# The last 512 tokens of a four-layer sequence model as two chunks of 256, with the later layers as one stream beside the later attention

## The chip, the cores and the metric

The kernel runs on one core of a Trainium2 chip. The metric is the device time of one execution in microseconds (us); three runs were timed, and the median is quoted. Beside these there is one profiled execution, whose trace gives start, duration and cause of waiting of every instruction. The engines are called as the profile calls them: PE (TensorE matmul) and PEld (its weight loads), DVE (VectorE), ACT (ScalarE), POOL (GpSimd) and SP (SyncE, which here only issues DMAs).

## The reference

The input `x` has 2 sequences of 1024 tokens with 256 features, all in f32. Four layers follow one another, each adding to `x`; the kernel normalizes the tokens (layer norm) ahead of each.

```
attention   16 heads of 128; softmax(min/max-clipped q.k/sqrt(128) + causal mask + slope_h * key) v, then Wo
ternary FFN weights rounded to -1/0/1 times a scale per group of 64; silu(g) * u, rms norm, projection 1024 -> 256
state space in-projection 256 -> 2 x 512, causal convolution over 4 tokens, silu; delta = softplus(...);
            for 512 channels x 16 states:  h[t] = exp(delta[t] a) h[t-1] + delta[t] B[t] x[t];  y[t] = sum_n C[t] h[t]
            y gated by silu(z), out-projection
2:4 FFN     silu(g) * u with 1024 hidden units; of every four the two of largest magnitude are kept; projection
```

Attention needs all earlier tokens of its sequence (keys and values), the state space needs the state and three convolution inputs of the token before. The other layers work on each token by itself.

## The kernel before

**Chunks.** The 2048 tokens are cut into four chunks of 512, `CH = [(0,0),(0,1),(1,0),(1,1)]` (sequence, half). `x[k]` stays in SBUF. A chunk's attention must be finished for all 16 heads before its other three layers, `rest(k)`, can begin.

**Attention** (`attention`, L382) is a generator that goes through the heads of all chunks in order and yields after each tile of 128 queries. For one tile, `scores` (L355) multiplies q with all keys so far (`s`, L362), clips and masks on DVE (`ss`, L366), adds the slope and finds the extreme (`nm`, L372, DVE, reads `ss` and `alibi` from SBUF), and exponentiates on ACT (L377). Two tiles later `turn` (L293) transposes the tile on PE, and a copy on ACT or DVE (`pT`, L296) brings it back; when a head's four tiles are turned, `values` (L304) and one tile later `project` (L318, L324 on DVE) follow. `qkv` (L335, L342) makes the next head's q, k, v during the second tile. Keys and values of a sequence's first half are written to DRAM (`kd`, `vd`) and loaded again for each head of the second half (L282, L283). A head's four weights, its slope row, and the old keys and values are loaded by SP (L267 to L283), each as soon as a buffer is free.

**The other layers** are generators too. `ternary_ffn` (L451), `state_space` (L517) and `kept_two_ffn` (L885) yield numbers that stand for cost. The state space has 64 products per chunk, one for each of 4 channel groups and 16 states, each on tiles of 128 channels x 512 tokens: SP loads rows of B and C from DRAM to all partitions (`bs`, `cs`, L691), POOL makes `db` = du * bs (L736), ACT makes `da` = exp (L750) into PSUM, DVE scans (`hs`, L757) and keeps the last column as `carry` (L766), POOL weighs `hc` = hs * cs (L771), and PE adds `hc` into `y` by transposing matmuls (L701). For the last chunk (`tail_end`) `db` is made by PE instead, with diagonal matrices (L730) or scaled copies (L724), so that POOL has only `hc`.

**Order.** The first attention chunk runs beside the quantizing of the ternary weights. Then, for k = 1, 2, 3, the tiles of attention k are dealt out against `rest(k-1)` in proportion to the yielded costs, a product counting 2.2, and what is left of `rest(k-1)` is emptied before the next chunk:

```
for k in range(1, len(CH)):
    r, done = rest(k - 1), 0.0
    for i in range(H * UT):
        next(heads)
        whole = cost(k - 1)
        while done < whole * (i + 1) / (H * UT):
            done += next(r, whole)
    for _ in r:
        pass
```

`rest(3)` runs alone at the end. To fill its gaps, the four last projections of `rest(2)` are held back (`held`, `fill_in`) and handed out there. A scheduler turns this order of emission into one order per engine, and allocates buffers from pools with a fixed number of each tag; each engine then works strictly in its order.

Of the kernel before, what the change touches and what calls it, by code (L numbers as in the profile page):

```python
# [17 lines left out]
P = 128  # L18
# [11 lines left out]
U = 512  # L30
UT = U // P
NU = S // U
# [9 lines left out]
def kernel(  # L42
# [28 lines left out]
    def bank(tag, bufs):  # L71
        return lambda name, dt=F32: ps.tile([P, 512], dt, tag=tag, name=name, bufs=bufs)
# [6 lines left out]
    CH = [(b, u) for b in range(B) for u in range(NU)]  # L79
    x = []  # L80
    for k in range(len(CH)):
        x.append(const.tile([P, UT, D], F32, name=f"x{k}"))

    def load_x(k):
        b, u = CH[k]
        src = x_in[b, u * U : (u + 1) * U, :].rearrange("(t p) d -> p t d", p=P)
        if k:
            nc.sync.dma_start(out=x[k], in_=src)
        else:

            for t in range(0, UT, 2):
                (nc.scalar if t else nc.sync).dma_start(out=x[k][:, t : t + 2, :], in_=src[:, t : t + 2, :])
# [19 lines left out]
    def layernorm_T(k, key, put, bank):  # L112
# [4 lines left out]
        step = 2 if k == len(CH) - 1 and key[0] != "a" else UT  # L117

        def turn_two(i):
            if i and step == 2:  # L120
                fill_in()
            tp = bank(f"lnp_{key}_{i}").rearrange("p (c t) -> p c t", c=KC)
            for j in range(2):
# [9 lines left out]
            put(slice(i * P, (i + 2) * P), tp)  # L133

        for i in range(UT):
# [3 lines left out]
            if (i + 1) % step == 0:  # L139
# [3 lines left out]
                for j in range(done.start, done.stop, 2):  # L143
                    turn_two(j)

    def plain(pool, key):
        xT = pool.tile([P, KC, U], F32, tag="xT", name=f"xT_{key}")
        return xT, lambda t, p: nc.any.tensor_copy(xT[:, :, t], p)  # L148
# [78 lines left out]
    def normed(k):  # L227
        xns[k], put = plain(a2, f"a{k}")
        layernorm_T(k, f"a{k}", put, ps_mm)
# [32 lines left out]
    def load_head(k, h):  # L262
        b, u = CH[k]
# [8 lines left out]
        n = (u + 1) * U  # L272
# [7 lines left out]
        if u:  # L280
            kd, vd = kept.pop((b, h))
            nc.sync.dma_start(out=w["kT"][:, :U], in_=kd)  # L282
            nc.sync.dma_start(out=w["v_all"][:, :UT, :], in_=vd)  # L283
        return w

    def turn(k, h, j, s, st):

        qi = CH[k][1] * UT + j
# [9 lines left out]
    def values(k, h, st):  # L298
        u = CH[k][1]
        zp = ps_z(f"z_{k}_{h}")  # L300
        last = (u + 1) * UT - 1
        for kb in range(last + 1):
            q0 = max(0, kb - u * UT) * P
# [4 lines left out]
        st["z"] = a2.tile([P, U], F32, tag="z", name=f"zs_{k}_{h}")  # L308
        nc.any.tensor_copy(st["z"], zp)  # L309

    def project(k, h, st):

        rr = a3.tile([P, UT], F32, tag="rr", name=f"rr_{k}_{h}")
        nc.vector.reciprocal(rr, st["rs"])
        for t in range(0, UT, 2):
# [12 lines left out]
    def qkv(k, h, st, xT):  # L328
        u = CH[k][1]
        st["qT"] = a2.tile([P, U], F32, tag="qT", name=f"qT_{k}_{h}")  # L330
        kT = st["kT"][:, u * U : (u + 1) * U]
        for n, dst, scale in (("q", st["qT"], -1.0 / math.sqrt(DH)), ("k", kT, 1.0)):
            pp = ps_mm(f"p{n}_{k}_{h}")
# [5 lines left out]
        vp = ps_mm(f"pv_{k}_{h}").rearrange("p (t m) -> p t m", t=UT)  # L339
        for t in range(UT):  # L340
# [5 lines left out]
        v = st["v_all"][:, u * UT : (u + 1) * UT, :]  # L346
        nc.any.tensor_copy(v, vp)
        if u < NU - 1:
            kd = dr.tile([P, U], F32, tag="kd", name=f"kd_{k}_{h}", bufs=H)
            nc.sync.dma_start(out=kd, in_=kT)  # L350
            vd = dr.tile([P, UT, DH], F32, tag="vd", name=f"vd_{k}_{h}", bufs=H)
            nc.sync.dma_start(out=vd, in_=v)
            kept[CH[k][0], h] = kd, vd

    def scores(k, h, j, st):  # L355

        W = (CH[k][1] * UT + j + 1) * P
# [24 lines left out]
    def attention():  # L382
# [7 lines left out]
        for i, (k, h) in enumerate(heads):  # L390
            st = live.pop(0)
            if i + 1 < len(heads):
                live.append(load_head(*heads[i + 1]))
            u = CH[k][1]
            st["pts"] = [
                a3.tile([P, 4, U], F32, tag="pT", name=f"pT_{k}_{h}_{i}") for i in range(u + 1)
            ]
            st["rs"] = a3.tile([P, UT], F32, tag="rs", name=f"rs_{k}_{h}")
            for j in range(UT):
                s = scores(k, h, j, st)  # L400
                later.append((LAG, lambda a=(k, h, j, s, st): turn(*a)))
                if j == UT - 1:
                    later.append((LAG, lambda a=(k, h, st): values(*a)))
                    later.append((LAG + 1, lambda a=(k, h, st): project(*a)))
                if j == UT - 1 and h == H - 1:
# [8 lines left out]
                if j == 1 and i + 1 < len(heads):  # L414
                    qkv(*heads[i + 1], live[0], xns[heads[i + 1][0]])
                if j == 0 and h == H - 1 and k + 1 < len(CH):

                    with tc.issue_after(tiles[-UT].ins) if k == 0 else nullcontext():
                        normed(k + 1)
                yield k  # L420
# [14 lines left out]
    def glu(pool, key, xTs, g_of, u_of, ic, h, bank=ps_r):  # L435

        g_ps, u_ps = bank(f"g_{key}_{ic}"), ps_r(f"u_{key}_{ic}")
# [7 lines left out]
        sg = pool.tile([P, U], F32, tag="sg", name=f"sg_{key}_{ic}", bufs=2)  # L445
# [5 lines left out]
    def ternary_ffn(k):  # L451
        with ExitStack() as fctx:
# [8 lines left out]
            x2 = [fc.tile([P, KC, U], F32R, name=f"x{i}_{k}") for i in "hl"]  # L461
# [7 lines left out]
            h2 = [fc.tile([P, NFC, U], F32R, name=f"h{i}_{k}") for i in "hl"]  # L469
            ss = fc.tile([P, U], F32, name=f"ss_{k}")  # L470
            for ic in range(NFC):
                h = f2.tile([P, U], F32, tag="h", name=f"h_{k}_{ic}")
# [7 lines left out]
                lower = nc.vector if k == len(CH) - 1 else nc.gpsimd  # L480
# [3 lines left out]
                else:  # L484
                    sq = f2.tile([P, U], F32, tag="sq", name=f"sq_{k}_{ic}")
# [4 lines left out]
            for t in range(UT):  # L490
# [4 lines left out]
            inv = f2.tile([P, UT], F32, tag="inv", name=f"inv_{k}")  # L495
            nc.vector.tensor_scalar(inv, sp[:, :UT], 1.0 / FF, RMS_EPS, ALU.mult, ALU.add)
            nc.gpsimd.tensor_tensor(inv, inv, minus_half[:, :UT], ALU.pow)
            for t in range(UT):
# [18 lines left out]
    def state_space(k):  # L517
        b, u = CH[k]
        first, last, tail_end = u == 0, u == NU - 1, k == len(CH) - 1
# [3 lines left out]
        with ExitStack() as mctx:  # L523
# [3 lines left out]
            xs = mc.tile([P, NDC, U], F32, name=f"xs_{k}")  # L527
            sz = mc.tile([P, NDC, U], F32, name=f"sz_{k}")
            dtl = mc.tile([P, U], F32, name=f"dtls_{k}")
            work = lambda name: mc.tile([P, U], F32, tag="cv", name=name, bufs=2)  # L530
            diag = mc.tile([P, DN, UT, P], F32, name=f"diag_{k}") if tail_end else None
# [6 lines left out]
            bcd = dr.tile([2, DN, U], F32, tag="bcd", name=f"bcd_{k}", bufs=2)  # L538

            row_of = lambda tag, name, bufs: mc.tile([P, U], F32, tag=tag, name=name, bufs=bufs)  # L540
# [3 lines left out]
            def steps(c):  # L544

                vp = ps_r(f"dt_{k}_{c}")
# [30 lines left out]
            def turned(c, du):  # L577

                tp = ps_r(f"dup_{k}_{c}")
                for t in range(UT):  # L580
# [8 lines left out]
            with ExitStack() as ictx:  # L589
# [11 lines left out]
                xT, put = plain(mi, f"m{k}")  # L601
# [3 lines left out]
                def in_proj(e):  # L605
                    pp = (spare(k) if e % 2 else ps_r)(f"in_{k}_{e}")
# [7 lines left out]
                for e in range(NDC):  # L614
                    xp = mi.tile([P, DC - 1 + U], F32, tag="xp", name=f"xp_{k}_{e}", bufs=2)
# [5 lines left out]
                    if not last:  # L621
                        nc.gpsimd.tensor_copy(tail[:, e, :], xp[:, U:])
                    acc = work(f"cv_{k}_{e}")
                    nc.vector.tensor_scalar(acc, xp[:, 0:U], cw(e, 0), None, ALU.mult)
                    for i in range(1, DC):
                        nc.vector.scalar_tensor_tensor(
                            acc, xp[:, i : i + U], cw(e, i), acc, op0=ALU.mult, op1=ALU.add
# [9 lines left out]
                dl_ps = ps_r(f"dtl_{k}")  # L637
# [8 lines left out]
                bc_ps = ps_da(f"bcp_{k}")  # L646
# [8 lines left out]
                bc = mi.tile([2 * DN, U], F32, name=f"bc_{k}", padded_shape=[P, U])  # L655
# [3 lines left out]
                if tail_end:  # L659
                    turns[0] = turned(0, parts[0][1])  # L660

                    bT_ps = ps_da(f"bT_{k}")[:, : UT * 2 * DN].rearrange("p (t n) -> p t n", t=UT)
# [385 lines left out]
```

## Time and profile before

| | |
|---|---|
| timed runs | 1835.65 us median (1833.6, 1835.65, 1840.51) |
| profiled execution, first to last instruction (span) | 1836.9 us, inside the range of the timed runs |
| instructions | 24217 |
| busy: PE / DVE / ACT / POOL | 94% / 66% / 52% / 45% of the span |
| mean granted clock of PE | 0.989 of full |
| DMA | 255.99 MB, 139 GB/s on average |

From the start times of the instructions, the span falls into these stages. Attention 0 ends at about 236 us, attention 1 at 733, attention 2 at 1121, attention 3 at 1606. The scans (L757) of the four chunks run from 345 to 564, from 823 to 997, from 1234 to 1452, and, in the last stage without attention, from 1672 to 1776. Busy time of PE is an average that hides these stages: a matmul's end is modelled, and a run of matmuls counts as busy from the first to the last.

### The profile page before, as it was taken

What the parts mean: (1) busy time and instruction counts of PE and PEld (TensorE: products, weight loads), DVE (VectorE), ACT (ScalarE), POOL (GpSimd) and SP (SyncE); (2) the same over time, 40 slices, a digit from 0 to 9 for tenths busy, and PEclk for the clock granted to TensorE, in tenths of its full rate; (3) what the DMA queues carried; (4) which work ended last, traced back from release to release, by engine and by line L of the source; (5) the groups of instructions that cost most, each with busy time, mean ns of one, the idle gap of its engine ahead of it and who ended that gap; (6) DMA issues with size and microseconds to landing.
All of it is one profiled execution on the core that took longest, in us unless ns stands there. A gap on an engine that the chain in (4) does not pass through costs nothing. (4 is left out here: it accounts for less than half of the span.)

```text
span 1836.9 us, 24217 instructions
## 1 busy us (share of the span) xinstructions
PE 1718.3 (94%) x7956; PEld 1144.2 (62%) x7956; DVE 1218.3 (66%) x2349; ACT 963.7 (52%) x1789; POOL 832.2 (45%) x674
## 2 busy tenths in 40 slices
PE   7999999998999999998888999999999999998899
PEld 4666666555656557755555667756656565566895
DVE  5666555777785473458886565557788655667975
ACT  3444474656563553555554545566555446446742
POOL 3324032588892000419998000418898500035870
PEclk9999999999999999999999999999999999999999
DMA  6443512466662311337787324227665430212541
GB/s 201 128 142 128 193 46 88 149 203 204 216 202 91 103 52 48 125 109 232 245 247 224 116 71 141 82 67 228 226 214 184 142 115 26 75 53 86 178 136 57
DMA packets 178301, 255.99 MB, mean 139 GB/s; under 512 B 16240, under 2 KB 90992, under 8 KB 177152
## 3 DMA queue, kind: packets, MB, share of 16 engines
q1 hardware_dynamic: 176752, 241.61, 41.4%
q0 software_dynamic: 1152, 12.58, 1.9%
q8 instruction: 63, 1.03, 0.2%
q14 instruction: 62, 0.51, 0.1%
q10 hardware_dynamic: 272, 0.26, 0.0%
HBM read 232.04 MB, written 22.35 MB: 138 GB/s over the span
## 5 line engine op out<-in xcount | busy, mean ns | idle before, releaser
L771 POOL TENSOR_TENSOR hc<-hs,cs 128x512 f32<-128x512 f32 x256 | 362.1, 1428 | 10.8 <-DVE ss L366 3.1
L362 PE MATMUL s<-kT,qT 128*128 128x512 f32 (+3 forms) x768 | 302.7, 495 | 19.9 <-DVE ss L366 18.0
L377 ACT ACTIVATE ss<-ss,nm 128x128 f32<-128x128 f32 (+7 forms) x256 | 198.8, 776 | 183.5 <-DVE nm L372 174.1
L366 DVE SCALAR_TENSOR_TENSOR ss<-s,lower 128x512 f32<-128x512 f32 (+3 forms) x384 | 204.6, 549 | 121.0 <-PE s L362 119.4
L736 POOL TENSOR_TENSOR db<-du,bs 128x512 f32<-128x512 f32 x192 | 259.2, 1356 | 44.4 <-DVE hs L757 30.6
L304 PE MATMUL z<-pT,v 128*128 128x512 f32 (+3 forms) x768 | 264.5, 492 | 10.9 <-ACT pT L296 10.2
L372 DVE CUSTOM_DVE_ANT_0 ss<-ss,alibi 128x128 f32<-128x128 f32 (+7 forms) x256 | 241.3, 945 | 3.5
L750 ACT ACTIVATE da<-dl,a_neg 128x512 f32<-128x512 f32 x256 | 177.9, 698 | 115.6 <-DVE hs L757 90.6
L304 PEld LDWEIGHTS z<-pT,v 128*128 128x128 f32 x768 | 142.8, 190 | 145.1 <-issue 92.7
L296 ACT COPY pT<-pt 128x512 f32<-128x512 f32 (+3 forms) x321 | 145.4, 474 | 162.0 <-PE pt L293 160.4
L293 PE MATMUL pt<-ident,ss 128*128 128x128 f32 x1152 | 180.3, 279 | 32.1 <-DVE x L324 18.5
L293 PEld LDWEIGHTS pt<-ident,ss 128*128 128x128 f32 x1152 | 140.0, 142 | 94.7 <-DVE x L324 33.0
L362 PEld LDWEIGHTS s<-kT,qT 128*128 128x128 f32 x768 | 127.9, 193 | 84.1 <-issue 43.4
L757 DVE TENSOR_TENSOR_SCAN hs<-da,db 128x512 f32<-128x512 f32 x128 | 153.8, 1210 | 38.6 <-ACT da L750 20.8
L757 DVE TENSOR_TENSOR_SCAN hs<-da,carry,db 128x512 f32<-128x512 f32 x128 | 159.1, 1269 | 24.4 <-POOL hc L771 14.7
L324 DVE SCALAR_TENSOR_TENSOR x<-o,rr,x 128x256 f32<-128x256 f32 x256 | 108.9, 476 | 76.7 <-PE o L318 76.5
L701 PE MATMUL y<-ident,hc 128*128 128x128 f32 x1024 | 144.8, 279 | 8.4 <-POOL hc L771 8.4
L342 PEld LDWEIGHTS pv<-wv,xT_a 128*128 128x128 f32 x1024 | 124.4, 192 | 37.1 <-issue 25.3
L342 PE MATMUL pv<-wv,xT_a 128*128 128x128 f32 x1024 | 125.8, 275 | 5.5 <-ACT zs L309 3.4
L701 PEld LDWEIGHTS y<-ident,hc 128*128 128x128 f32 x1024 | 121.0, 145 | 14.3 <-POOL hc L771 11.9
L318 PE MATMUL o<-wo,zs 128*128 128x256 f32 x512 | 125.4, 386 | 4.1 <-ACT kT L338 3.0
L335 PE MATMUL pq<-xT_a,wq 128*128 128x512 f32 x256 | 122.7, 601 | 0.7 <-ACT xT_a L148 0.7
(204 smaller groups left out, 2468.7 us busy)
## 6 DMA issues: line engine op xcount, KB each, us to landing
cs<-bcd SPq DMA_DIRECT2D x256, 256.0 KB, 3.8
bs<-bcd SPq DMA_DIRECT2D x192, 256.0 KB, 4.3
alibi<-alibi_d SPq DMA_DIRECT2D x32, 512.0 KB, 4.2
wq<-in_wqT_dram SPq DMA_DIRECT2D x64, 128.0 KB, 3.5
wk<-in_wkT_dram SPq DMA_DIRECT2D x64, 128.0 KB, 3.1
wv<-in_wvT_dram SPq DMA_DIRECT2D x64, 128.0 KB, 2.8
wo<-in_woT_dram SPq DMA_DIRECT2D x64, 128.0 KB, 2.8
alibi<-alibi_d SPq DMA_DIRECT2D x32, 256.0 KB, 3.6
```

Source lines behind the costliest of these rows:

```text
L293: nc.tensor.transpose(tp[:, i, :], s[:, (kb0 + i) * P : (kb0 + i + 1) * P], ident)
L304: nc.tensor.matmul(zp[:, q0:], lhsT=st["v_all"][:, kb, :], rhs=st["pts"][kb // 4][:, kb % 4, q0:], start=(kb == 0), stop=(kb == last),)
L342: nc.tensor.matmul(vp[:, t, :], lhsT=xT[:, c, t * P : (t + 1) * P], rhs=st["v"][:, c, :], start=(c == 0), stop=(c == KC - 1),)
L362: nc.tensor.matmul(sp[:, :n], lhsT=st["qT"][:, j * P : (j + 1) * P], rhs=st["kT"][:, k0 : k0 + n], start=True, stop=True,)
L366: nc.vector.scalar_tensor_tensor(s[:, k0 : k0 + n], sp[:, :n], CLIP, lower[:, S - W + k0 : S - W + k0 + n], op0=ALU.min, op1=ALU.max,)
L372: pace["tile"] = nc.vector.tensor_tensor_reduce(out=s[:, :W], in0=s[:, :W], in1=st["alibi"][:, :W], scale=1.0, scalar=3.0e38, op0=ALU.add, ...
L377: nc.scalar.activation(s[:, :W], s[:, :W], AF.Exp, bias=nm, scale=-1.0, accum_out=st["rs"][:, j : j + 1])
L701: nc.tensor.matmul(yTs[c][:, t * P : (t + 1) * P], lhsT=h[:, t * P : (t + 1) * P], rhs=ident, is_transpose=True, start=start and t == 0, s ...
L736: nc.gpsimd.tensor_tensor(db[i], du, brow.pop(i), ALU.mult)
L750: nc.scalar.activation(da[i], parts[c][0], AF.Exp, scale=a_neg[:, c, n : n + 1])
L757: nc.vector.tensor_tensor_scan(out=hs[i], data0=da.pop(i), data1=db.pop(i), initial=0.0 if first else carry[:, n, c : c + 1], op0=ALU.mult ...
L771: nc.gpsimd.tensor_tensor(hc[i], hs.pop(i), crow.pop(i), ALU.mult)
```

## The change

Five chunks in place of four: the last 512 tokens become two chunks of 256, each with its own attention (16 heads of two tiles), its own three layers, and all tiles cut to 256 columns. `CH` now holds (sequence, first tile, tiles). Keys and values of one sequence share one DRAM buffer, and the fifth chunk loads 768 old tokens of them. `rest(3)`, of the first 256, is an ordinary chunk: it runs beside attention 4, and its `db` is made by POOL. Only `rest(4)`, of the last 256, runs alone at the end in the `tail_end` form; the held projections are the two of `rest(3)`.

From `rest(1)` on, the layers are one queue: what attention 2 leaves of `rest(1)` goes on beside attention 3, and so on to the end of attention 4. Each attention chunk takes a share of the whole cost in proportion to its work, and a product now counts 5.0 there (2.2 in `rest(0)`, whose pace against attention 1 is as it was).

```diff
-NU = S // U
+CH = [(0, 0, UT), (0, UT, UT), (1, 0, UT), (1, UT, UT // 2), (1, UT + UT // 2, UT // 2)]
...
-        step = 2 if k == len(CH) - 1 and key[0] != "a" else UT
+        ut = CH[k][2]
+        step = ut // 2 if k == LAST and key[0] != "a" else ut
...
-        if u:
-            kd, vd = kept.pop((b, h))
-            nc.sync.dma_start(out=w["kT"][:, :U], in_=kd)
-            nc.sync.dma_start(out=w["v_all"][:, :UT, :], in_=vd)
+        if t0:
+            kd, vd = kept[b, h]
+            nc.sync.dma_start(out=w["kT"][:, : t0 * P], in_=kd[:, : t0 * P])
+            nc.sync.dma_start(out=w["v_all"][:, :t0, :], in_=vd[:, :t0, :])
...
-                if j == 1 and i + 1 < len(heads):
-                    qkv(*heads[i + 1], live[0], xns[heads[i + 1][0]])
...
+                if j == ut // 2 - 1 and i + 1 < len(heads):
+                    qkv(*heads[i + 1], live[0], xns[heads[i + 1][0]])
...
-            part = lambda tag, name, bufs: m2.tile([P, U], F32, tag=tag, name=name, bufs=bufs)
+            part = lambda tag, name, bufs: m2.tile([P, w], F32, tag=tag, name=name, bufs=bufs)
...
-                    yield 2.2
+                    yield PRODUCT(k)
...
+    PRODUCT = lambda k: 2.2 if k == 0 else 5.0
+
     def rest(k):
-        yield from ternary_ffn(k)
-        yield from state_space(k)
-        yield from kept_two_ffn(k)
+        part = CH[k][2] / UT
+        for layer in (ternary_ffn, state_space, kept_two_ffn):
+            for step in layer(k):
+                yield step * part
...
+    work = lambda k: H * sum(32 + 10 * (CH[k][1] + j + 1) for j in range(CH[k][2]))
+    units, done, later = [], 0.0, range(2, len(CH))
+
+    def layers(until):
+        nonlocal done
+        while units and done < until:
+            step = next(units[0], None)
+            if step is None:
+                units.pop(0)
+            else:
+                done += step
+
     for k in range(1, len(CH)):
-        r, done = rest(k - 1), 0.0
-        for i in range(H * UT):
+        units.append(rest(k - 1))
+        if k == 1:
+            share = cost(0)
+        else:
+            share = sum(cost(i - 1) for i in later) * work(k) / sum(work(i) for i in later)
+        begun, steps = done, H * CH[k][2]
+        for i in range(steps):
             next(heads)
-            whole = cost(k - 1)
-            while done < whole * (i + 1) / (H * UT):
-                done += next(r, whole)
-        for _ in r:
-            pass
+            layers(begun + share * (i + 1) / steps)
+        if k in (1, LAST):
+            layers(math.inf)
```

All other lines of the diff replace the width 512 by the chunk's own width `w`, and the four tiles by its own number `ut`.

## Prediction

> **What bounds the kernel now.** I read the page first, for the shares of the engines over the span, and then asked for busy times stage by stage, because the shares differ between stages.
>
> ```profile
> PE   7999999998999999998888999999999999998899
> POOL 3324032588892000419998000418898500035870
> ```
>
> The two lines are busy tenths in 40 slices of 46 us. PE is at 9 nearly everywhere, and POOL comes in four bursts: the products of the four chunks. The windows are cut at the first and last scan of each chunk (us busy, number of instructions):
>
> ```profile
> core 0: us, PE busy (x) PEld busy (x) DVE busy (x) ACT busy (x) POOL busy (x), PEclk, DMA share, GB/s
> 0.00:345.00 345.00, 327.48 (x1475) 211.80 (x1476) 211.85 (x552) 179.10 (x374) 92.52 (x107) 1.00 0.40 126
> 345.00:564.00 219.00, 201.69 (x971) 132.31 (x970) 174.58 (x304) 126.29 (x229) 191.18 (x137) 1.00 0.67 209
> 564.00:823.00 259.00, 254.74 (x1066) 161.78 (x1064) 136.12 (x306) 130.65 (x231) 30.78 (x30) 1.00 0.25 81
> 823.00:998.00 175.00, 141.37 (x710) 100.42 (x709) 145.82 (x208) 93.99 (x193) 170.58 (x131) 0.93 0.78 241
> 998.00:1234.00 236.00, 232.59 (x974) 151.04 (x973) 126.81 (x290) 121.37 (x213) 35.10 (x37) 0.98 0.30 98
> 1234.00:1453.00 219.00, 202.03 (x973) 132.41 (x971) 173.98 (x305) 127.28 (x231) 192.08 (x137) 1.00 0.65 210
> 1453.00:1606.00 153.00, 147.57 (x585) 89.44 (x586) 81.19 (x160) 72.68 (x121) 4.30 (x4) 1.00 0.21 72
> 1606.00:1672.00 66.00, 62.19 (x260) 41.84 (x259) 39.23 (x80) 31.55 (x53) 15.54 (x16) 0.97 0.13 41
> 1672.00:1776.00 104.00, 92.77 (x754) 87.42 (x753) 97.11 (x83) 68.10 (x131) 96.61 (x76) 0.97 0.51 162
> 1776.00:1837.00 61.00, 55.84 (x205) 35.75 (x202) 31.59 (x69) 12.65 (x20) 3.50 (x4) 1.00 0.18 63
> ```
>
> Between the products PE is busy 96 to 98.5% of the time. Beside long attention (345 and 1234) PE has 202 of 219 us and POOL 191. Beside short attention (823) POOL is the bound, 171 of 175 us, and PE has 34 us free. In the last stage, 1606 to 1837, no engine waits long either: PE 211 of 231 us, and from 1672 DVE and POOL 97 of 104.
>
> **The change, first in PE's own work.** PE streams by columns: four 512-wide f32 records of `pq` follow one another in 1.71 us (1055.42 to 1057.13), eight 256-wide ones of `o` in 1.73 (173.18 to 174.91), so 0.43 and 0.216 us each, and a transpose of 128 takes 0.112. Halving the width therefore costs PE nothing, and the causal blocks of attention are the same. A tile of 128 queries costs 7.0/4 = 1.74 us for q, k, v and `o`, and 0.54 us per key block (0.215 `s`, 0.112 turn, 0.215 `z`): about 3.1 us in attention 2, 4.7 and 5.8 in the two halves of attention 3. What goes is half of the diagonal `db` of the last stage (416 and 48 records, 58.5 + 7.8 us busy): -33 us of 1718. PE has less to do, and still the place decides. The last stage is 231 us for 512 tokens; half of its layers now lie beside attention, where PE is already over 92% busy.
>
> **The last stage, for 256 tokens.** 1606 to 1672: 62 us of PE work become about 31, but the chain into it (last `x` at 1607, first `g_f` at 1613.2) and the like chain ahead of the in-projection do not shrink: 44. The products need the price of narrow instructions:
>
> ```profile
> L366 DVE SCALAR_TENSOR_TENSOR ss<-s,lower 128x512 f32<-128x512 f32 x192 | 130.2, 682 | 69.1 <-PE s L362 67.9
> L366 DVE SCALAR_TENSOR_TENSOR ss<-s,lower 128x256 f32<-128x256 f32 x64 | 26.6, 415 | 11.5 <-PE s L362 11.2
> L771 POOL TENSOR_TENSOR hc<-hs,cs 128x512 f32<-128x512 f32 x63 | 94.9, 1511 | 2.8 <-DVE ss L366 1.5 <-PE y L701 1.3
> L771 POOL TENSOR_TENSOR hc<-hs,cs 128x512 f32<-128x512 f32 x61 | 81.7, 1343 | 0.0
> L771 POOL TENSOR_TENSOR hc<-hs,cs 128x512 f32<-128x512 f32 x63 | 79.8, 1308 | 2.1 <-DVE hs L757 1.8
> ```
>
> The first two lines are one DVE operation at two widths (mean ns last before the bar): 148 ns are constant, so a scan of 1270 ns should become 710. The three `hc` lines are the windows from 345, 823 and 1672. No line shows POOL at 256 columns. Half of the wide one, 0.67 us, is the floor; a copy of three columns on POOL takes 0.30, and a constant of that size would give 0.82; all of that added to half would be 0.99. I take 0.82 beside attention and 0.79 alone. Then 64 scans are 45 us, DVE's diagonals and the rest 11; POOL has 64 x 0.79 + 11 = 62, the later of the two: 104 becomes 62. The end, 61 us with 56 of PE, becomes 34: half of PE, and 6 us of chain. Together 140, a gain of 91.
>
> The Trainium skill ("Perfetto Trace Analysis", Optimizing Scalar/DVE Operations) says that each Scalar or DVE operation carries a constant, some 125 ns on PSUM for DVE, and that larger ones are better where the engine is saturated: a rule against this change. Our row says 148. On the 249 instructions that DVE gains, it is 37 us by the row and 31 by the page, and DVE is in neither case the bound.
>
> **Beside attention.** The order of the instructions on each engine, which is fixed when the kernel is built, tells what stands between the first and last product of each chunk. Chunk 0 is as before, so the first 564 us stay. The next gap has 8 us less attention in it: 259 becomes 252.
>
> Chunk 1's products now have 43 tiles beside them (31 before): PE 30 for `y`, 4 for steps and gates and 132 for tiles, 166 us; POOL 64 x (1.35 + 1.36) + 4, about 177. PE alone would take 166 x 219/202 = 180, POOL alone 177/0.975 = 181. Two engines that are both full wait for one another, so I take 187: 12 more than before.
>
> The gap behind it loses 54 us of attention: 236 - 54 = 182. The cover is thinner: picking the two largest (L924, L880 to L882) is some 18 us of DVE alone, which some 4 tiles hid and now 2.5 hide. I add 6: 188.
>
> Chunk 2's products have 27 tiles, in heads of two: PE 173 (30 + 139 + 4), POOL between 171 and 192, by the two windows. Again both full: 194.
>
> The gap up to chunk 3's products holds 152 us of PE work, by the rows above; at the 96% of the window from 1453, 159.
>
> Chunk 3's products, the first 256 of the last 512 tokens, have only 7 tiles beside them, because a product of half the width still counts half of 5.0: PE has 63 us. POOL has both multiplications again: 128 x 0.82 + 9 x 0.82 = 112. This is the heart of my forecast: a stretch of 112 us in which PE has 50 us free. At POOL prices of 0.67 and 0.99 it is 92 or 136. What is left of the chunk and of attention, 48 us of PE, takes 53.
>
> The sum: 564 + 252 + 187 + 188 + 194 + 159 + 112 + 53 + 140 = 1849, against 1836.9 of the profiled execution, which lies 1.2 above the median of 1835.65. In terms of the median I say 1848. The 91 us won at the end are spent again, 103 us, beside attention, because the stage that moved is now bound by POOL.
>
> **Queues.** SP issues 16 more sets of four weights, slope, keys and values, and 64 + 128 rows of half size in place of 64 of full size. Keys and values wait in its queue for a buffer, and the rows of B and C stand behind them:
>
> ```profile
> SPq L283 <- PE z L304: 183.6, 18, 22.1
> ```
>
> That is 18 waits of 184 us in all, the longest 22. POOL is five rows ahead, 5 x 2.7 = 13.5 us before, and 5 x 1.6 = 8 us with half tiles. POOL's wait for rows was 5.4 us in the window from 823 and 6.4 in that from 345; I leave it in the ratios above. A second wait is new: in heads of two tiles, q, k, v of the next head come before `z` of the head before, whose `v` buffer they need; on PE `pv` stands ahead of that `z`, so the copy of `v` (L347) waits for one of the two 128-query steps, and one PSUM bank of three is held that long. Behind the copy on ACT stand `da` and the exponentials. I cost it at nothing, since the scheduler puts the copy where `z` is done; if that cover fails it is up to 1 us for each of 32 heads.
>
> The three `hc` lines also say that POOL is slower beside attention, by 200 ns against the last stage: 13 us per chunk with 31 tiles. In the Trainium skill ("SBUF — State Buffer", Who interferes with whom), a DVE instruction with two SBUF inputs contends with a GpSimd instruction that reads SBUF, as `nm` (L372) does; a full lock for 43 tiles of some 1 us would put up to 43 us on POOL.
>
> **The rivals.** *Faster:* the single queue keeps every stage full. The trace shows that POOL alone can run at 97.5%, with PE served beside it. If narrow POOL instructions cost 0.67 us (stretch of 3: 94, last products 54), the two full stages run at POOL's 180 and 183, and the thinner gaps stay at 98.5% of PE (182 and 154), the sum is 564 + 252 + 180 + 182 + 183 + 154 + 94 + 53 + 132 = 1794; with half of these, about 1820. It decides from a narrow `hc` under 0.72 us. Against it: 202 + 191 us of two engines took 219 in both windows where both were full.
>
> *Nothing:* PE loses 33 us, idle POOL-bound time grows as much; within 9 us of 1836. It needs only 12 us off my sum, for instance POOL at 0.76.
>
> *Much slower:* rows late in SP's queue. With 17 heads in the stretches of chunks 2 and 3, in place of 8, 2 us each for a starved POOL make 34 us: 1882. It shows as POOL `db` waiting for DMA `bs` by tens of us.
>
> That the change does not do what it says is excluded by the order: 64 `db` of 256 columns stand on POOL, and the diagonals on PE are halved.
>
> **How the numbers follow.** Forecast, slower by 10 to 25 us: 0.40. Much slower: 0.12. Nothing: 0.20. Faster: 0.28. What a measurement of this kernel can tell from no change is about 0.5%, 9 us: slower than 1845 has 0.52, between 0.20, faster than 1826.5 has 0.28. The range goes from 1805, inside the faster case, to 1888, past the starved POOL and POOL's upper price (+24 and +13 us on the sum); the forecast's own range is 1842 to 1866.
>
> **What would show it.** In the profile after: the last stage near 140 us; a stretch without much PE work at some 1545 to 1655 where POOL is at 9 and PE at 6; narrow `hc` and `db` near 0.8 us; products of chunk 1 at 187 us and chunk 2 at 194, PE and POOL both near 9. I am wrong if the last stage is over 160 or under 125, if narrow POOL work is under 0.7, or if PE stays over 90% through chunk 3's products.

## Result, and the profile after

| | median of the timed runs | span of the profiled execution |
|---|---|---|
| before, same chip | 1836.68 us (1833.6 to 1840.51, 4 runs) | 1836.9 us |
| after | 1926.28 us (1922.23 to 1929.83, 4 runs) | 1928.1 us |

The ratio is 1.0485, 95% interval 1.0464 to 1.0507: slower by 89 us (the ratio times 1837; the two medians differ by 89.6). The forecast said slower, but 1848, and its range ended at 1888.

The same two lines of the page of after, 40 slices of 48 us:

```profile
PE   7999999999999999979899999877789998769887
...
POOL 3323040798860003198882022777771024971282
```

POOL now has five bursts. In the third and fourth PE drops to 7 and 6, and POOL is at 7 too in the third: there both wait for something. The windows of after, cut at the first and last scan of each chunk (us busy, number of instructions):

```profile
core 0: us, PE busy (x) PEld busy (x) DVE busy (x) ACT busy (x) POOL busy (x), PEclk, DMA share, GB/s
...
564.00:823.00 259.00, 252.59 (x1052) 161.10 (x1052) 130.65 (x293) 127.94 (x225) 31.74 (x32) 0.99 0.26 84
823.00:1021.00 198.00, 170.44 (x851) 118.05 (x852) 168.59 (x262) 109.73 (x233) 171.23 (x131) 0.95 0.72 230
1021.00:1220.00 199.00, 191.41 (x821) 131.64 (x820) 107.86 (x242) 90.19 (x170) 35.81 (x37) 0.97 0.36 117
1220.00:1453.00 233.00, 185.96 (x935) 145.16 (x934) 164.66 (x300) 108.58 (x215) 177.30 (x133) 0.90 0.75 230
1453.00:1629.00 176.00, 172.81 (x827) 127.81 (x828) 99.04 (x201) 82.75 (x151) 27.89 (x38) 1.00 0.45 151
1629.00:1739.00 110.00, 78.26 (x354) 52.34 (x353) 81.35 (x181) 53.83 (x121) 97.54 (x133) 0.86 0.63 192
1739.00:1791.00 52.00, 48.72 (x240) 37.90 (x239) 29.69 (x65) 21.76 (x41) 4.94 (x7) 1.00 0.35 115
```

From 1791 to 1928 the last 256 tokens run alone. Against the terms of the prediction:

| stage of after | predicted | measured |
|---|---|---|
| to the end of chunk 0's products | 564 | 564 |
| gap | 252 | 259 |
| chunk 1's products | 187 | 198 |
| gap | 188 | 199 |
| chunk 2's products | 194 | 233 |
| gap | 159 | 176 |
| products of the first 256 | 112 | 110 |
| rest beside attention | 53 | 52 |
| last stage | 140 | 137 |

The windows of before that the prediction starts from begin 3 to 7 us ahead of the first scans, which start at 349.8, 825.7, 1239.0 and 1678.8 us; those of after begin at them. So its terms for the products of chunks 1 and 2 hold some 3 and 5 us that the table counts in the gaps ahead of them.

The totals of the first 256 and of the last stage came out right, and so, nearly, did the price of narrow POOL work. Here are the 256-wide lines of after, the first two beside attention, from 1629 to 1739, the third from the last stage (mean ns last before the bar):

```profile
L754 POOL TENSOR_TENSOR db<-du,bs 128x256 f32<-128x256 f32 x63 | 48.5, 771 | 11.4 <-DMA bs<-bcd 9.7 <-DVE carry L784 1.7
L789 POOL TENSOR_TENSOR hc<-hs,cs 128x256 f32<-128x256 f32 x61 | 47.5, 779 | 0.0
```

```profile
L789 POOL TENSOR_TENSOR hc<-hs,cs 128x256 f32<-128x256 f32 x61 | 43.2, 745 | 4.4 <-DVE hs L775 2.2 <-PE y L719 1.4 <-DMA cs<-bcd 0.7
```

What went wrong lies in chunks 1 and 2 and the gaps between. The waits of POOL from 1220 to 1453, the products of chunk 2 (engine, line, what it waited for, us, times, longest):

```profile
POOL hc L789 <- DMA cs<-bcd: 27.3, 8, 5.2
POOL db L754 <- DMA bs<-bcd: 19.3, 12, 4.0
```

That is 46.6 us of POOL standing for rows of B and C. Before, from 1239 to 1453, no wait of POOL for a row is among its waits; the largest is for a scan:

```profile
POOL db L736 <- DVE hs L757: 17.1, 4, 5.9
```

Why the rows are late stands in SP's own waits, of before and then of after, in the same stretch:

```profile
SPq L691 <- POOL hc L771: 81.3, 56, 2.9
SPq L691 <- POOL db L736: 32.5, 25, 3.3
SPq L283 <- PE z L304: 10.5, 2, 10.2
```

```profile
SPq L291 <- PE z L312: 33.8, 7, 9.2
SPq L365 <- ACT kT L348: 31.7, 7, 5.9
SPq L291 <- PE s L375: 10.3, 5, 3.0
SPq L709 <- POOL hc L789: 5.5, 6, 2.4
```

Before, SP stood 114 us at the rows themselves, waiting for POOL to free a buffer: it was ahead of POOL, and the waiting cost nothing. After, it stands 44 us at the loads of `v` (L291), 34 of them for a `z` that still reads the buffer, and 32 us at the stores of `kT` (L365), which wait for ACT's copy; at the rows it waits for POOL only 10 us in all (L709: 5.5 for `hc`, 4.7 for `db`). SP is behind, and POOL waits for it.

The chain of waits that ended last, on the page of after, has the rows in its list (shares of the span):

```profile
DMA bs<-bcd 4%; PE z L312 3%; DMA cs<-bcd 3%; POOL hc L789 3%; POOL db L754 3%; PE u_g L456 2%; PE g_g L456 2%; PE s L375 2%; PE go L953 2%; PE pq L345 1%; DVE hs L775 1%; PE pk L345 1%; PE y L719 1%; PE o L327 1%; PE pt L301 1%
```

From 1220 to 1453 this chain goes through transfers of rows for 77 us, counted from issue to landing. So the late rows are on the path, not beside it. The list of before can't be set against this one: its chain can be followed back only to 1579 us, into the end of attention 3, and says nothing of chunk 2's products.

A second count, an estimate, tells how much is lost, and where. It takes PE's records at the rates at which they follow one another in these traces (0.43 us for 512 columns, 0.216 for 256, 0.112 for a transpose; 0.23 and 0.12 for the 512 and 256 columns of `g_f`, `u_f` and `fo`). By it PE has 1653 us of work before and 1627 after, so it idles 184 and 301 us. Of the 117 more, 54 are in chunk 2's products (21.5 before, 75.4 after), 52 in the products of the first 256, which did not exist, and 11 in all the rest, where chunk 1's products idle less than before (49, then 41). The count takes PE at its full clock. The granted clock was 0.90 and 0.86 in the first two of these stretches, so up to some 18 and 9 us of what is called idle there can be slower matmuls (158 and 58 us of work, divided by these shares).

### The profile page after: what moved, and what is told of

Its sections match the earlier page's. It is cut to its first block, busy times and chain, and to the rows that moved or that the text cites. A ratio compares the mean times of both kernels' runs of the same rounds, so it can differ in the third digit from the quotient of the medians.

```text
span 1928.1 us, 26087 instructions
## 1 busy us (share of the span) xinstructions
PE 1744.8 (90%) x8218; PEld 1214.7 (63%) x8218; DVE 1258.6 (65%) x2598; ACT 969.1 (50%) x1930; POOL 895.3 (46%) x844
## 4 chain that ended last, share of the span: by engine, by line
PE 24%; DMA 10%; POOL 7%; DVE 5%; issue 4%; ACT 3%; SPq 1%; POOLq 0%; DVEq 0%; ACTq 0%
DMA bs<-bcd 4%; PE z L312 3%; DMA cs<-bcd 3%; POOL hc L789 3%; POOL db L754 3%; PE u_g L456 2%; PE g_g L456 2%; PE s L375 2%; PE go L953 2%; PE pq L345 1%; DVE hs L775 1%; PE pk L345 1%; PE y L719 1%; PE o L327 1%; PE pt L301 1%
## 5 line engine op out<-in xcount | busy, mean ns | idle before, releaser
L789 POOL TENSOR_TENSOR hc<-hs,cs 128x512 f32<-128x512 f32 (+1 forms) x320 | 369.8, 1166 | 54.4 <-DMA cs<-bcd 36.8
L754 POOL TENSOR_TENSOR db<-du,bs 128x512 f32<-128x512 f32 (+1 forms) x256 | 305.5, 1198 | 81.0 <-DMA bs<-bcd 39.1
L312 PE MATMUL z<-pT,v 128*128 128x512 f32 (+1 forms) x960 | 280.0, 438 | 25.5 <-ACT pT L304 20.6
L768 ACT ACTIVATE da<-dl,a_neg 128x512 f32<-128x512 f32 (+1 forms) x320 | 192.8, 609 | 157.4 <-DVE hs L775 123.8
L312 PEld LDWEIGHTS z<-pT,v 128*128 128x128 f32 x960 | 181.6, 195 | 137.8 <-issue 58.5
L385 DVE CUSTOM_DVE_ANT_0 ss<-ss,alibi 128x128 f32<-128x128 f32 (+7 forms) x256 | 257.7, 1009 | 3.4
L719 PE MATMUL y<-ident,hc 128*128 128x128 f32 x1024 | 168.5, 289 | 53.5 <-POOL hc L789 51.4
L775 DVE TENSOR_TENSOR_SCAN hs<-da,carry,db 128x256 f32<-128x256 f32 (+1 forms) x192 | 170.5, 914 | 26.6 <-POOL db L754 15.3
L345 PE MATMUL pq<-xT_a,wq 128*128 128x512 f32 (+1 forms) x320 | 132.9, 539 | 8.1 <-DMA wq<-in_wqT_dram 5.4
L352 PE MATMUL pv<-wv,xT_a 128*128 128x128 f32 x1024 | 130.9, 278 | 1.7 <-DVE zs L317 1.0
```

Of the source, the lines that this page charges most:

```text
L312: nc.tensor.matmul(zp[:, q0:], lhsT=st["v_all"][:, kb, :], rhs=st["pts"][kb // 4][:, kb % 4, q0:], start=(kb == 0), stop=(kb == last),)
L352: nc.tensor.matmul(vp[:, t, :], lhsT=xT[:, c, t * P : (t + 1) * P], rhs=st["v"][:, c, :], start=(c == 0), stop=(c == KC - 1),)
L385: pace["tile"] = nc.vector.tensor_tensor_reduce(out=s[:, :W], in0=s[:, :W], in1=st["alibi"][:, :W], scale=1.0, scalar=3.0e38, op0=ALU.add, ...
L719: nc.tensor.matmul(yTs[c][:, t * P : (t + 1) * P], lhsT=h[:, t * P : (t + 1) * P], rhs=ident, is_transpose=True, start=start and t == 0, s ...
L754: nc.gpsimd.tensor_tensor(db[i], du, brow.pop(i), ALU.mult)
L768: nc.scalar.activation(da[i], parts[c][0], AF.Exp, scale=a_neg[:, c, n : n + 1])
```

## Experiments

Two theories came first. Q: the rows stand in SP's queue behind loads and stores of two-tile heads. S: the single stream, with a product counted at 5.0, packs two engines too full and leaves the gaps thin. Four kernels test them.

**Stream alone.** Four chunks as before, everything else as in the change:

```
-CH = [(0, 0, UT), (0, UT, UT), (1, 0, UT), (1, UT, UT // 2), (1, UT + UT // 2, UT // 2)]
+CH = [(0, 0, UT), (0, UT, UT), (1, 0, UT), (1, UT, UT)]
```

> Four chunks of 512 again, with the later layers as one queue and a product counted at 5.0. Theory Q (SP's queue: in the changed kernel, rows of B and C stand behind the loads and stores of keys and values of heads of two tiles) expects no heads of two tiles, so no starved POOL: POOL waits for rows under 15 us in all, chunk 2's products 215 to 225 us, total 1825 to 1850. Theory S (the single queue itself fills the stages too densely, and PE, DVE and POOL wait for one another) expects most of the loss here too: 1880 to 1930.

Measured: 1847.98 us, ratio to before 1.0054 (1.0034 to 1.0074). S is refuted as the main cause: the stream is worth 10 us of 89. Q's total came (1825 to 1850) and its waits too (of POOL's waits there only 6 us are put down to a DMA at all), but not its stage: chunk 2's products took 231 us, not 215 to 225.

**Split alone.** Five chunks, each chunk's layers emptied beside the next attention, a product at 2.2:

```
-    PRODUCT = lambda k: 2.2 if k == 0 else 5.0
+    PRODUCT = lambda k: 2.2
...
-        if k == 1:
-            share = cost(0)
+        if k:
+            share = cost(k - 1)
...
-        if k in (1, LAST):
+        if k:
```

> Five chunks, but each chunk's layers are emptied beside the next attention as in the kernel before, with a product counted at 2.2 everywhere. Q expects chunk 2's products beside about 8 heads of two tiles in place of 14: waits for rows about half of the 47 us, but products bound by POOL with PE idle, 190 to 200 us; total 1880 to 1910. S expects the loss gone with the single queue: 1835 to 1860.

Measured: 1943.5 us, ratio 1.0567 (1.0536 to 1.0599). The split costs the time, and without the stream it costs more than Q said (1880 to 1910), though the stage came as Q had it: chunk 2's products took 194 us, and POOL waited 18 us there for rows.

**The queue, relieved in two steps.** First the stores of the first 256 tokens' keys and values are issued by ACT, then the loads of `v` as well:

```
+            store = nc.scalar if k == 3 else nc.sync
-            nc.sync.dma_start(out=kd[:, t0 * P : t0 * P + w], in_=kT)
-            nc.sync.dma_start(out=vd[:, t0 : t0 + ut, :], in_=v)
+            store.dma_start(out=kd[:, t0 * P : t0 * P + w], in_=kT)
+            store.dma_start(out=vd[:, t0 : t0 + ut, :], in_=v)
... second step, also:
-            nc.sync.dma_start(out=w["v_all"][:, :t0, :], in_=vd[:, :t0, :])
+            (nc.scalar if k > 2 else nc.sync).dma_start(out=w["v_all"][:, :t0, :], in_=vd[:, :t0, :])
```

> The changed kernel; the stores of chunk 3's keys and values to DRAM are issued by ACT in place of SP (SP's pauses ahead of them were 36 us in 1220 to 1453). Q expects POOL's waits for rows to fall from 47 to about 25 us there, and the total to fall by 10 to 25 us, to 1900 to 1915. S expects no change beyond 5 us.

> As the run before, and the loads of old values for chunks 3 and 4 are issued by ACT too, so that SP does not wait for z (46 us of pauses in 1220 to 1453). Q expects POOL's waits for rows under 10 us in chunk 2's products, these products at 195 to 205 us, and the total at 1880 to 1900. S expects 1920 to 1930. A loss on ACT, which then waits for z itself, would show as ACT idle behind z and as 1930 or more.

Measured: 1919.69 us (ratio 1.0418, 1.0375 to 1.046), then 1907.18 (1.0368, 1.0335 to 1.0401): 7 and 19 us back, less than Q expected both times. Chunk 2's products of the second step, its window, SP's largest wait there and POOL's:

```profile
1220.00:1425.00 205.00, 169.51 (x887) 132.69 (x885) 162.59 (x302) 101.31 (x193) 176.15 (x132) 0.93 0.83 261
```

```profile
SPq L710 <- POOL hc L790: 43.8, 30, 4.4
```

```profile
POOL db L755 <- DMA bs<-bcd: 20.6, 6, 7.6
```

The stage fell from 233 to 205 us, SP waits for POOL again, and DMA moves 261 GB/s where it moved 230. So the rows were not late for lack of bandwidth; they stood in SP's queue. They are not all in time now: with 1.0 us for `cs` POOL still stands 21.6 us for rows, where Q expected under 10 (27.8 after the first step, where Q expected 25). Of the stage's 28 us the whole kernel keeps 19: fewer tiles lie beside the shorter stretch, and the next gap grew from 176 to 183. Q has a mechanism that costs time here, and it explains about a fifth of the loss.

A new theory for the rest, N: the narrow layers themselves cost it. The first 256 tokens' products are bound by POOL while PE idles, beside too few tiles. The rival was Q again, in the traffic of the two-tile heads wherever they are.

**Attention split alone.** The heads run as in the change, in two passes of two tiles for the last 512 queries, with all loads and stores. The layers stay in four chunks:

```
+AC = [(0, 0, UT), (0, UT, UT), (1, 0, UT), (1, UT, UT // 2), (1, UT + UT // 2, UT // 2)]
+CH = [(0, 0, UT), (0, UT, UT), (1, 0, UT), (1, UT, UT)]
... attention's functions read AC in place of CH; the order of emission:
+    for k in range(1, len(AC)):
+        if k < len(CH):
+            units.append(rest(k - 1))
```

> Only attention is split: the last 512 queries go through the 16 heads in two passes of two tiles (with all stores and loads of keys and values that the change adds), while the layers stay in four chunks of 512, in one stream. Theory Q (the queue and the traffic of the two-tile heads cost the time): most of the 78 us that lie between the stream alone (1848) and the change (1926) come here too, 1895 to 1920. Theory N (the narrow layers cost it: the first 256 tokens' products are bound by POOL, 110 us with 50 us of PE unfilled, and the last 256 pay the chain between layers once more): 1850 to 1865.

> The run before with the stores of chunk 3's keys and values, and the loads of v for the last 512 queries, issued from ACT. Q: the 19 us that this gave to the change, or more, come back: 20 to 40 us under the run before, if that is at 1895 to 1920. N: there is little to give back, within 8 us of the run before, 1845 to 1860.

Measured: 1853.51 us (ratio 1.0091, 1.007 to 1.0112), and with the relieved queue 1854.43 (1.0095, 1.0079 to 1.0112). Both are in N's range and far from Q's: sixteen more loads of all the old keys and values, sixteen more sets of weights, cost 7 us over the stream alone. The second run is a control too: moving these transfers to ACT is worth nothing by itself. POOL's waits for rows in chunk 2's products, of the first run (two lines) and of the second:

```profile
POOL db L758 <- DMA bs<-bcd: 25.4, 13, 5.2
POOL hc L793 <- DMA cs<-bcd: 5.6, 3, 4.2
```

```profile
POOL db L759 <- DMA bs<-bcd: 6.6, 6, 3.9
```

With wide layers, then, 31 us of late rows became 7 (8 more are put down to a load of `wo`), and the time did not change: a wait for rows is not by itself a loss. That it is one in the change may come from the stores, of which ten heads' fall into chunk 2's products there and three heads' here; no run tests this.

**More tiles beside the narrow products.** The relieved kernel (1907 us), with a product of the first 256 counted double:

```
-    PRODUCT = lambda k: 2.2 if k == 0 else 5.0
+    PRODUCT = lambda k: 2.2 if k == 0 else 10.0 if k == 3 else 5.0
```

> The change with stores and v loads on ACT (1907), and a product of the first 256 tokens counted at 10.0 in place of 5.0, which at half width is 5.0 a product, so that about twice as many tiles of attention lie beside the stretch of 110 us. N: PE's 50 free us there are used, some 40 us of attention move in and half of it is won: 1875 to 1895. Q: each of these tiles brings loads into the stretch, rows come late there too, and what moves in lengthens it by as much: 1902 to 1925.

Measured: 1909.68 us, ratio 1.04 (1.0375 to 1.0426). N's expectation failed, and the time lies in Q's range (1902 to 1925), though not for Q's reason: POOL waited 7.7 us for rows in that stretch, and 6.8 before the edit. The stretch with more tiles (PE first, POOL last of the engines):

```profile
1571.00:1698.00 127.00, 113.33 (x593) 86.08 (x591) 106.78 (x238) 72.25 (x157) 102.09 (x133) 0.99 0.74 230
```

The tiles did move in: the stretch took 127 us in place of 109 with, by the estimate of PE's work, 91 us of attention beside it in place of 43, and PE idled 21 us there in place of 50. But its idle time over the whole kernel is 280 us, against 277: chunk 1's products now idle 52 us (41), and from the end of the narrow products to the last scans PE idles 36 us (16), since more of the first 256 tokens' layers then ran after attention had ended. This other deal of the same attention moved the holes and did not remove them.

**A quarter of the multiplications by C on DVE**, in the first 256 tokens of the change itself:

```
+                weigher = nc.vector if k == 3 and i % 4 == 3 else nc.gpsimd
-                nc.gpsimd.tensor_tensor(hc[i], hs.pop(i), crow.pop(i), ALU.mult)
+                weigher.tensor_tensor(hc[i], hs.pop(i), crow.pop(i), ALU.mult)
```

> The change itself, with every fourth multiplication by C of the first 256 tokens (16 of 64) made by DVE in place of POOL. N: POOL is the bound of that stretch, 12 us less of it make 110 about 99 us, and the time 1912 to 1920. Q: the stretch is not where the time went, and the rest is as it was: 1922 to 1932.

Measured: 1923.91 us, ratio 1.0471 (1.0446 to 1.0496). The median lies in Q's range (1922 to 1932) and outside N's (1912 to 1920), but the interval, 1919 to 1928 us, reaches both, and the change itself: the run does not decide. The stretch went from 110 to 103.5 us, 6.5 of the 11 us expected; POOL's busy time fell 7 us there in place of 12, for this reason (groups of POOL and of DVE in that stretch):

```profile
L754 POOL TENSOR_TENSOR db<-du,bs 128x256 f32<-128x256 f32 x63 | 50.7, 811 | 11.4 <-DMA bs<-bcd 11.4
L790 POOL TENSOR_TENSOR hc<-hs,cs 128x256 f32<-128x256 f32 x46 | 37.1, 807 | 0.1
```

```profile
L790 DVE TENSOR_TENSOR hc<-hs,cs 128x256 f32<-128x256 f32 x15 | 11.0, 734 | 0.0
```

POOL's own multiplications became 4 to 5% slower, and DVE needed nearly as long as POOL for the same multiplication.

**POOL's second multiplication taken away.** The relieved kernel, where the first 256 tokens' scans read delta*x, without the multiplication by B and its rows (part of the computation is left out):

```
-                    if a == 0 and by_tensor(i):
+                    if a == 0 and (by_tensor(i) or k == 3):
                         return
...
+                if k == 3:
+                    db[i] = du
-                if tail_end and by_scalar(n):
+                elif tail_end and by_scalar(n):
```

> The change with stores and v loads on ACT (1907), in which the first 256 tokens' products leave out the multiplication by B: the scan reads delta*x itself, so 64 multiplications of POOL and 64 rows are gone, and nothing takes their place. Theory N (POOL's two multiplications set the length of that stretch, 109 us): DVE with 84 us busy there is the next bound, the stretch takes 84 to 92 us, and the time is 1880 to 1892. Theory M (the stretch only hides what attention and the layers around it would take anyway): within 8 us of 1907.

Measured: 1882.3 us, ratio 1.0239 (1.0207 to 1.027): 25 us off 1907, as N said (24 by the ratios, since the two runs are of two chips). The stretch, with PE and POOL in the same columns as above, for the relieved kernel and then without B:

```profile
1608.00:1717.00 109.00, 78.66 (x357) 54.23 (x356) 83.68 (x188) 52.13 (x116) 97.49 (x135) 0.84 0.65 198
```

```profile
1616.00:1699.00 83.00, 68.03 (x362) 50.40 (x361) 74.76 (x186) 52.64 (x119) 54.80 (x73) 0.96 0.59 173
```

26 us shorter, and now DVE is the fullest, 75 of 83. So what B costs in this stretch was on the path. The run takes the multiplication and its rows away together, but POOL had waited only 5.2 us for `bs` there and now has 43 us less to do: POOL's work, more than the rows, had set the length.

**Can the order be improved in the kernel before?** From the stretches seen I expected attention to be cheaper beside chunk 1's products than between products. The kernel before, with that chunk's product at 5.0, and at 3.5:

```
-                    yield 2.2
+                    yield PRODUCT(k)
...
+    PRODUCT = lambda k: 5.0 if k == 1 else 2.2
... and in the sum of costs, PRODUCT(k) in place of 2.2
```

> The kernel before, with a product of chunk 1 counted at 5.0 in place of 2.2, all others at 2.2: more of attention 2 lies beside chunk 1's products, where PE idled 50 us. From the stretches seen so far (171 us with 90 us of attention beside, 186 with 102, 198 with 125, 224 with 158: 0.78 us for each us of attention, and 1.03 between the products): some 65 us of attention move, 1815 to 1828. If thin cover between the products costs as much as it wins, 1833 to 1842.

> The same with 3.5: some 35 us of attention move; 1824 to 1833 by the stretches, 1833 to 1842 if thin cover takes it back.

Measured: 1841.8 us (ratio 1.0017, 1.0003 to 1.0031) and 1854.32 (1.0083, 1.0059 to 1.0106). The expectation failed (1815 to 1828, then 1824 to 1833). The first time lies where thin cover takes the gain back (1833 to 1842), the second beyond that too. Chunk 1's products, of before, at 5.0 and at 3.5 (PE first, POOL last of the engines):

```profile
823.00:998.00 175.00, 141.37 (x710) 100.42 (x709) 145.82 (x208) 93.99 (x193) 170.58 (x131) 0.93 0.78 241
```

```profile
822.00:1015.00 193.00, 164.72 (x793) 111.87 (x794) 159.19 (x245) 103.39 (x217) 170.34 (x133) 0.93 0.74 232
```

```profile
822.00:1016.00 194.00, 156.43 (x746) 106.93 (x745) 154.38 (x221) 100.47 (x207) 166.05 (x129) 0.90 0.73 221
```

POOL's busy time stays near 170. From first to last scan the stretch takes 172, 193 and 194 us. At 5.0 it grows 22 us for 23 us more of attention (113 against 90), and PE idles 48 us of it as it did (49, by the estimate). At 3.5 it grows as much for 14 us, and PE idles 59. I had fitted 0.78 us per us of attention through stretches of different kernels; within one kernel most or all of it was paid. No version that ran beats the kernel before.

## Why the prediction was wrong

**The loss by parts.** These parts follow one path through the runs. Each ratio is to before on the same chip, taken times 1837 us: the stream +0.54%, 10 us; two-tile heads, by the run with attention split alone, +0.37%, 7 us; narrow layers, by the relieved kernel against the same heads with layers of 512, from 1.0095 to 1.0368, 50 us; the queue, from 1.0368 to 1.0485, 21 us. With 1 us between the two runs of split attention these are the 89 us. The intervals of these ratios are 3 to 6 us to each side, so the queue's 21 us and the 19 between the two medians are one number.

**The failed step** is the term of chunk 2's products, 194 us for 233, and in it the sentence that leaves POOL's 5.4 and 6.4 us for rows "in the ratios above". The wait was 46.6 us. The prediction had the parts in hand: SP's queue holds loads that wait for buffers, 16 more sets of them, and POOL's reserve of five rows. It even counted heads, 17 in place of 8, but only for the rival "much slower"; its own sum gave late rows nothing new. Within chunk 2's products SP issued 13 loads of old keys, where it had issued 8, and the stores of 10 heads, where there had been none: two-tile heads come twice as often per tile, and only those of the first 256 both load and store. With the relieved queue the stage took 205 us: 28 of the 39 us are gone, some 8 of them because less of PE's work lay there (150 us in place of 158, by the estimate). 11 us over the term remain, with POOL still waiting 21.6 us for rows. Of the whole miss of 79 us (1928 for 1849) this term has 39, chunk 1's products and the three gaps have 46, and 6 came back.

The rival "much slower" named this mechanism, with `db` waiting for `bs` by tens of us, and priced it at 34 us on a sum without other misses. The trace has 46.6 in chunk 2's products (27.3 of it `hc` waiting for `cs`) and 9.7 in the next. Its 1882 was low because the other terms failed as well.

**The gaps and chunk 1.** PE's work was about right: chunk 1's products and the gap behind them have 339 us of it for 348 predicted, chunk 2's and the gap behind 326 for 325. What was short is idle time: 27 allowed for the first pair and 58 measured, 28 and 83 for the second. The term that failed here is "Two engines that are both full wait for one another, so I take 187", and the 194 and the gaps worked out like it. "Both full" cannot be read as one ratio of busy times. From 345 to 564 PE and POOL ran at 0.92 and 0.87 of the window, and in chunk 1's products after at 0.86 and 0.86. DVE, which the term leaves out, was busy 169 of 198 us there, 0.85: three engines were nearly full, not two. Whether that is the reason no run shows. Slower POOL work was not: `hc` took 1365 ns there, 1343 before. The halved diagonals saved PE 26 us by the estimate, not 33, and a narrow scan took DVE 743 ns, not 710.

**Right, in part by luck:** the heart of the forecast is right in kind, a stretch bound by POOL with PE idle, but that its 112 us came so near the 110 measured is two errors that cancel. The 112 stood for POOL's work alone, at 0.82 us; that work took 97.5 us, at 0.77 and 0.78, and POOL waited for most of the rest, 9.7 us of it for `bs`, which the term did not have. The last stage, 140 us (137), is luck too: its parts were 44, 62 and 34 and measured 42, 54 and 41. Narrow POOL work alone was put at 0.79 us (0.75), and thin cover was named as a loss, though too small. The prediction's balance, 91 us won at the end and 103 spent beside attention, becomes 94 won (231 to 137) and 185 spent. Taking B away from the narrow products is worth 25 us; it would take more than that to make the change a gain.

**Open:** of the 50 us of the narrow layers those 25 are shown by a run, one that leaves work out. For the rest there is only the estimate of PE's work. Against the same heads with layers of 512, the relieved kernel has 27 us less of it and idles 76 us more: 14 in chunk 2's products, 44 between these and the last stage (the narrow products alone idle 50), 17 in the last stage, which pays the chain between layers for half the tokens. Chunk 1's products idle as much in both (41 and 43). Which wait holds PE in each is not settled.

## What to carry to other kernels

Work that is split in half and laid beside other work must find that work's holes still empty: the halved products made a further stretch bound by POOL, and the same attention could not fill three such stretches as it had filled two. Before splitting, count what each half issues again on a queue shared with someone's input: in this queue, which issues in order, a transfer that waits for a buffer holds those behind it, and whether SP waits for its consumer or the consumer for SP is read from who is named in SP's own waits. A ratio of busy times taken from one stretch doesn't carry to another with the same two engines.

## What the runs showed of the hardware

The multiplication of two 256-wide f32 tiles in SBUF took DVE 398 ns at best and 1043 at worst, 708 in the median, where POOL multiplied beside it; POOL's own went from 779 to 807 ns. The Trainium skill ("SBUF — State Buffer", Who interferes with whom) says that a DVE instruction with two SBUF inputs contends with a GpSimd instruction that reads SBUF; the spread of durations is in line with that, though no run here tells the cause. At these durations there was little point in giving DVE part of POOL's work.

Issuing 32 stores and 32 loads from ACT in place of SP gave 19 us in the change and nothing where the layers were wide. The Trainium skill ("DMA: Bandwidth & Descriptors", Issuing engines are not separate DMA queues) says that DMAs begun on several engines only save the sequencer's time to begin them. Here the sequencer's time was the point: in chunk 2's products SP spent some 108 us in its instructions and 125 us standing between them (from the start and end of each), which fills the window of 233. Before, in the 214 us from 1239, these were 91 and 123: it stood as long, but at the rows, behind POOL. In the relieved kernel they are 90 and 115 of 205. The run does not tell apart what the waits cost that went to ACT and what the 28 fewer issues on SP.

PE's granted clock was lower where PE waited: 0.90 in chunk 2's products and 0.86 in those of the first 256, with 1.00 in the gap between; in the run without B, where PE waited less, it was 0.96 in those of the first 256.
